# A four-layer stack on one core: stage ends in halves of the tokens, the last FFN in quarters, late gate norms issued before the experts end

## The chip, the cores and the metric

The kernel runs on one core of a Trainium2 chip. The metric is the time of one execution in device microseconds; lower is better. Engines in the profile: PE is TensorE, DVE VectorE, ACT ScalarE, POOL GpSimd, SP SyncE, which here only issues DMAs.

## The reference

x is (4, 512, 128) in float32. Eight blocks follow each other, each on a layernorm of x and added to x:

```python
x = x + _L0_attn_a_ref(_layernorm(x), ...)   # causal softmax attention, 16 heads of 8
x = x + _L0_ffn_ref(_layernorm(x), ...)      # mixture of 8 experts, top 2, and a shared one
x = x + _L0_attn_b_ref(_layernorm(x), ...)   # FAVOR+ linear attention
x = x + _L0_ffn_ref(_layernorm(x), ...)      # the same experts again
x = x + _L1_attn_a_ref(_layernorm(x), ...)   # gated linear attention, 8 heads of 64, own norm inside
x = x + _L1_ffn_ref(_layernorm(x), ...)      # FFN with blockwise FP4 rounding of inputs and weights
x = x + _L1_attn_b_ref(_layernorm(x), ...)   # retention, 16 heads, group norm
x = x + _L1_ffn_ref(_layernorm(x), ...)      # the same FP4 FFN again
```

The FP4 step, on blocks of 16 values of the last dimension, is what the FFN spends its VectorE and GpSimd time on:

```python
scale = jnp.max(jnp.abs(xb), axis=-1, keepdims=True) / 6.0
xn = xb / scale
q = _GRID[searchsorted(_MID, abs(xn))] * sign(xn) * scale   # grid 0, .5, 1, 1.5, 2, 3, 4, 6
```

It is applied to the normed input (512 tokens x 128) and to the product silu(gate) * up (512 x 352) of each batch. Retention's group norm averages over all 512 tokens of a batch, so nothing of a batch's second FFN can start before its retention is complete.

## The kernel before

x stays on the chip as one tile `X`; a batch is 512 tokens, in J = 4 blocks of 128. Softmax attention runs first, in an order written out by hand. Everything after it (about 240 us to the end) is cut into **streams**, one per batch and stage: the experts (`moe`, `shared`, `total`), `inward` and `favor`, `gates`, `keys` and `gated` for the gated attention, then `first` (FFN), `retention`, `leveled` (its group norm and output product) and `second` (FFN with store).

The order in which these are issued comes from a planner, `Clock` (L145). Streams are generators that yield what they wait for and how many PSUM banks they need. Work on ACT, DVE and POOL is registered by `later(engine, us, after, do)`, with a planned duration; whenever an operation's inputs are due it is issued. Among streams that can go on, the planner takes the one that can start first, and then the one with the higher number in the table `FAR` (L39). Engines run their instructions in exactly the planned order, so a waiting instruction holds up all behind it on its engine. The planner's times steer the order; nothing on the chip waits for them.

What the change and the steps of the prediction touch:

- `moments` (L326) computes mean and variance of a batch's four blocks: on DVE two instructions per block (L330, L331). `root_steps` (L305) is three Newton steps for 1/sqrt, on POOL (four instructions a step) or on DVE (three). `centred` (L333) applies scale and offset by four activations on ACT, one per block (L342).
- `add_x` (L402) adds a stage's result from PSUM to the batch's 128x512 of `X` in one DVE instruction (L403).
- `gates(b)` (L970) begins the gated attention: moments, roots on POOL, centring on ACT into `xn`, then transposes on PE (L382). For b = 0 and 1 the stream may start when the FAVOR stage's pools are free; for b = 2 and 3 (`EARLY` = 2) it starts only after the stream `experts`, i.e. when all expert work is issued. That stream runs `rest_pools` (L1115), which sets up the later stages and clears their buffers with five POOL memsets (L1569).
- `project` (L1080) is the gated attention's output product, 16 pairs of block and group into one bank.
- `normed` (L1574) is the norm ahead of `ffn` and `retention`: moments, roots and offset on DVE, centring on ACT.
- `quantized` (L1586) is the FP4 step: block maxima on DVE (L1594 to L1597), division on POOL (L1610), the power of two on DVE (L1600), a step on ACT (L1601), two rounding instructions on DVE (L1605, L1606), and the scale on POOL (L1612).
- `ffn` (L1616) handles a batch: norm, FP4 step on 128x512, transposes, gate and up products per block of 128 tokens, FP4 step on each half (two blocks, 128x704), then per block transposes (L1655), evacuation, down product, one add and, for `second`, one store of 256 KB.
- `leveled` (L1794) ends with four matmuls and one add.
- Retention's scores are masked on POOL, two instructions per head group (L1741).

The kernel also holds a second arm, taken only when decay values leave a range; the measured runs do not take it.

Of the kernel before, what the change touches and what calls it, by code (L numbers as in the profile page):

```python
# [14 lines left out]
ALU = mybir.AluOpType  # L15
# [15 lines left out]
UP = 1.0 + 2.0 ** -22  # L31
EXP, TANH, SILU = ("exp",), ("exp", "silu"), ("silu",)
EARLY = 2

# [4 lines left out]
FAR = {  # L39
    "moe": (34,),  # L40
    "shared": (589, 230, 101, 186, 338, 444, 196, 385),
    "total": (34, 334, 167, 440, 467, 482, 19, 193),
    "in": (0, 0, 100, 527, 450, 482, 45, 323),
    "inward": (364, 104, 384, 461),
    "favor": (378, 171, 133, 588),
    "gates": (135, 468, 451, 231),
    "keys": (237, 481, 541, 82),
    "gated": (377, 269, 540, 166),
    "first": (55, 466, 547, 542),
    "retention": (54, 134, 224, 459),  # L50
    "leveled": (326, 293, 76, 394),
    "second": (75, 76, 343, 438),
}
# [182 lines left out]
class Net:  # L236
    def __init__(self, ctx, tc, d):
# [16 lines left out]
        self.ident = self.k["ident"]  # L254
        self.quantized = None

# [68 lines left out]

    def moments(self, b, mv):  # L326

        for j in range(J):
            st = self.new(self.stat, [P, 6], "bn", bufs=4)
            self.nc.vector.bn_stats(st, self.xi(b * J + j))  # L330
            self.nc.vector.bn_aggr(mv[:, j, :], st)  # L331
# [69 lines left out]

    def add_x(self, b, ps):  # L402
        self.nc.vector.tensor_tensor(self.xb(b), self.xb(b), ps.rearrange("p (j d) -> p j d", d=P), ALU.add)  # L403

# [499 lines left out]
    def front(self, out):  # L904
# [5 lines left out]
        with ExitStack() as ctx, ExitStack() as now, self.tc.tile_pool(name="kept", bufs=1, space=bass.MemoryType.DRAM) as dram:  # L910
# [57 lines left out]
            xs, D, KD = {}, {}, {}  # L968

            def gates(b, clock, gp):  # L970

# [5 lines left out]
                def moments():  # L977
                    self.moments(b, mv[:, b])
                    v = self.new(self.stat, [P, 2, J], "v2")
                    nc.vector.tensor_scalar(v[:, 0], mv[:, b, :, 1], 1e-5, None, ALU.add)  # L980
                    nc.vector.tensor_scalar(v[:, 1], mv[:, b, :, 1], 1.0 + 1e-5, 1e-10, ALU.mult, ALU.add)
                    parts.append(self.root_steps(r12[:, b], v, "r12"))
                    next(parts[0])
# [4 lines left out]

                xn = []
                op = later("pool", 2.8, later("dve", 2.1, clock.since, moments), rest)  # L990
                op = later("act", 2.5, op, lambda: xn.append(self.centred(self.new(gp.mid, [P, J, P], "xn"), b, mv[:, b], r12[:, b, 1], own="g")))
                yield [op], "bank"
                ps = self.turned(xn[0])
# [86 lines left out]
            def project(b, pool, ot):  # L1080
                res = self.centred(self.new(pool, [P, J, P], "res"), b, mv[:, b], r12[:, b, 0], own="p")
                nc.gpsimd.tensor_tensor(self.xb(b), self.xb(b), res, ALU.add)
                ps = self.bank()
                for j in range(J):
                    for p in range(NG):
                        self.mm(ps[:, chunks[j]], ot[:, p, chunks[j]], wo[:, p * P:(p + 1) * P],
                                start=(p == 0), stop=(p == NG - 1))
                return ps

# [3 lines left out]
            with ExitStack() as over, self.banks():  # L1093
# [7 lines left out]
                nc.vector.tensor_scalar(nba, gs[:, :NG], -1.0, None, ALU.mult)  # L1101
                known = {}
                when = lambda *key: lambda: known.get(key)

# [10 lines left out]
                def rest_pools():  # L1115

                    now.close()
                    gp.late = tp(late, "late", 1)
                    gp.rest = self.rest(over, clock, D, KD, out)
                    clock.run("pool", 5.7, clock.since)  # L1120
                    yield 0.0
# [102 lines left out]
                for b in range(B):  # L1224
                    streams[f"inward{b}"] = ([f"favor{b - 2}"] if b >= 2 else [], None, lambda b=b: into(b), 460)
                    streams[f"favor{b}"] = ([f"inward{b}"], "favor", lambda b=b: featured(b), 400)
                    streams[f"gates{b}"] = (["pools" if b < EARLY else "experts"], None, lambda b=b: gates_of(b), 500 - 10 * b)
                    streams[f"keys{b}"] = ([f"gates{b}"] + [f"keys{b - 1}"] * (b > 0), None, lambda b=b: gp.keys(b), 495 - 10 * b)
# [35 lines left out]
    def chunked(self, arm, tp, clock, D, KD, fall, tri, wk, wv, rn, xs, queries, squares, keyed, of_heads, norms, project):  # L1264
# [108 lines left out]
        def steps(b):  # L1373
            yield from before(NG * b)
            done = []
            for u in range(NG * b, NG * (b + 1)):
                yield q[u], "bank", "bank"
                w = scores(u)
                if (u + 1) % NG:
# [3 lines left out]
            yield done, "bank"  # L1383
            ps = project(b, once, D[b])
            yield clock.later("dve", 0.7, [clock.pe(3.7), clock.later("pool", 1.4, clock.later("act", 2.0, clock.since))],
                              lambda: self.add_x(b, ps), "bank")

# [4 lines left out]
    def closed(self, arm, tp, wq, wk, wa, xs, by_token, project):  # L1392
# [87 lines left out]
        for b in range(B):  # L1480
# [3 lines left out]
            for p in range(NG):  # L1484
                attend(b, p, V, ot)
            self.add_x(b, project(b, sm, ot))

# [57 lines left out]
    def rest(self, arm, clock, D, KD, out):  # L1545
# [21 lines left out]
        of_head = va.rearrange("p (j g w) -> p j g w", j=J, w=wide)[:, :, :, :P].rearrange("p j g (i e) -> p j g i e", e=32)[:, :, :, :, :DH]  # L1567
        for t in (va, *ws):
            nc.gpsimd.memset(t, 0.0)  # L1569
        magic = self.new(one, [P, 1], "magic")  # L1570
# [3 lines left out]
        def normed(b, tag):  # L1574

            st, xn = {}, self.new(one, [P, J, P], tag)

            def moments():
                st["mv"] = self.new(self.stat, [P, J, 2], f"mvb{b}")
                self.moments(b, st["mv"])  # L1580
                st["r"] = self.rstd(st["mv"][:, :, 1], f"rstdb{b}", eng=nc.vector)

            op = later("dve", 4.5, clock.since, moments)
            return xn, later("act", 2.0, op, lambda: self.centred(xn, b, st["mv"], st["r"], nc.vector, f"{b}"))

        def quantized(dst, src, n, after, own):  # L1586

            sc, rc = (self.new(one, [P, n // BLK], t + own) for t in ("sc", "rc"))
            tmp = self.new(one, [P, n], "fw" + own)
            blk = lambda t: t.rearrange("p (n k) -> p n k", k=BLK)  # L1590
# [12 lines left out]
            def rounded():  # L1603

                stt(dst, tmp, MAGIC, dst, ALU.add, ALU.add)  # L1605
                stt(dst, tmp, MAGIC, dst, ALU.add, ALU.subtract)  # L1606

            u = n / T
            op = later("dve", 0.8 + 0.7 * u, after, scales)
            op = later("pool", 1.08 * u, op, lambda: nc.gpsimd.tensor_tensor(blk(dst), blk(src), _bc(rc, BLK), ALU.mult))  # L1610
            op = later("act", 0.1 + 0.5 * u, later("dve", 0.42 * u, op, power), number)
            return later("pool", 1.08 * u, later("dve", 1.36 * u, op, rounded), lambda: nc.gpsimd.tensor_tensor(blk(dst), blk(dst), _bc(sc, BLK), ALU.mult))  # L1612

        free = ["a", "b"]

        def ffn(b, store=False):  # L1616
            h, hq = room(KD[b])[:, :J * FF], room(D[b])[:, :J * FF]
            own = free.pop()
            xn, op = normed(b, "xn" + own)
            flat = xn.rearrange("p j d -> p (j d)")  # L1620
            op = quantized(flat, flat, T, op, own)
            yield op, "bank"
            ps = self.turned(xn)
            xT = self.new(one, [P, T], "fw" + own)
            ready = later("act", 0.6, pe(0.5), lambda: nc.scalar.copy(xT, ps), "bank")
            half = J * FF // 2
            halves, ended = [], []

# [15 lines left out]
            for j in range(J):  # L1644
                yield ready, "bank", "bank"
                gates(j)
                if j % 2:
                    c = slice(j // 2 * half, (j // 2 + 1) * half)
                    halves.append(quantized(hq[:, c], h[:, c], half, ended[-2:], f"{own}{j // 2}"))

# [13 lines left out]
            def down(j, hT):  # L1664
# [3 lines left out]
                return pe(0.65)  # L1668

            for i in range(2):  # L1670
                turns = []
                for j in (2 * i, 2 * i + 1):
                    yield halves[i], "bank"
                    turns.append(turn(j))
                for j in (2 * i, 2 * i + 1):
# [6 lines left out]
                    t = down(j, hT)  # L1682

            def add():
                self.add_x(b, po)
                if store:
                    nc.sync.dma_start(out.rearrange("(n p) d -> p n d", p=P)[:, b * J:(b + 1) * J, :], self.xb(b))

            yield later("dve", 0.65, t, add, "bank")
            free.append(own)  # L1690

# [3 lines left out]
        def retention(b):  # L1695
# [22 lines left out]
            for j in range(J):  # L1718
                self.mm(ps1[:, j, :], xs[:, chunks[j]], wv)
            of_v = later("act", 0.65, pe(0.95), lambda: nc.scalar.copy(of_head.rearrange("p j g i d -> p (j g) i d"), ps1.rearrange("p j (g i d) -> p (j g) i d", i=HG, d=DH)), "bank")  # L1720
            yield of_k, "bank"
# [72 lines left out]
        def leveled(b):  # L1794
# [24 lines left out]
            ps2 = self.bank()  # L1819
            for j in range(J):  # L1820
                self.mm(ps2[:, chunks[j]], y[:, chunks[j]], wo)
            yield later("dve", 0.65, pe(0.95), lambda: self.add_x(b, ps2), "bank")

# [29 lines left out]
```

## Time and profile before

| | us |
|---|---|
| median of 3 runs | 1032.96 (1032.49 to 1033.01) |
| the profiled execution | 1032.06 |
| its span, first to last instruction | 1030.3 |
| PE busy | 890.4 |
| DVE busy | 734.2 |
| ACT busy | 560.0 |
| POOL busy | 448.3 |

The costliest groups of the FFN and retention stages, from 640 us to the end, with count, busy time and mean:

| group | count | busy us | mean ns |
|---|---|---|---|
| POOL mask of retention's scores, 128x1024 (L1741) | 32 | 35.4 | 1122 |
| DVE moments per block (L330) | 56 | 14.9 | 267 |
| POOL FP4 division, 128x704 (L1610) | 8 and 8 | 12.1 and 11.8 | 1508 and 1478 |
| POOL FP4 scale, 128x704 (L1612) | 8 and 8 | 11.7 and 11.5 | 1458 and 1443 |
| DVE rounding, 128x704, first (L1605) | 8 and 8 | 7.5 and 7.4 | 944 and 926 |
| DVE rounding, 128x704, second (L1606) | 8 and 8 | 9.1 and 7.1 | 1133 and 893 |
| DVE add to X, 128x512 (L403) | 17 | 11.6 | 684 |

Where two numbers stand, they belong to the two sets of FFN buffers. A row of the timeline reads: start, duration, engine, line, operation, output from inputs, and in brackets how long the engine was idle before it and what released it. PSUM tiles are called `bank` throughout, and a line can be a helper's (L400 is every plain matmul), so groups are told apart by their tiles. Most matmuls stand in the trace as two records, so counts are twice those of the code.

### The profile page before, as it was taken

The page shows a single profiled execution, that of the slowest core. Times are in us where ns is not written, and L with a number is a line of the kernel's source. Part 1 is how long each engine was busy: PE and PEld are TensorE (multiplying, and loading weights), DVE is VectorE, ACT ScalarE, POOL GpSimd, SP SyncE. Part 2 cuts the span into 40 slices and gives each one's busy share as a digit, 9 for nine tenths or more (in the row PEclk, how much of TensorE's full clock was granted, in tenths as well). Part 3 has the DMA queues.
Part 4 walks back from the last instruction along what each step waited for, and adds up shares of the span by engine and source line. Part 5 has one row for each costly group of instructions (what it writes and reads, how often), then busy time and mean ns, then how long its engine had stood idle before and what let it go on. Part 6 is the DMA issues. An engine that isn't in the chain of part 4 may idle for free.

```text
span 1030.3 us, 17949 instructions
## 1 busy us (share of the span) xinstructions
PE 890.4 (86%) x6624; PEld 541.1 (53%) x6624; DVE 734.2 (71%) x1808; ACT 560.0 (54%) x1076; POOL 448.3 (44%) x899
## 2 busy tenths in 40 slices
PE   5999999998999989998988989678798977778734
PEld 3545555554335555444534457446687765566523
DVE  5657777755776898978877755596685864977664
ACT  3556656564774665757476742384345555465422
POOL 2434544341674554555556424463224515343322
PEclk9989999999999999999999999898998997997867
DMA  4000001000000000000000000100000000000000
GB/s 158 2 2 2 2 16 41 2 1 22 0 1 1 1 1 1 2 0 2 11 1 11 1 1 11 32 1 1 1 1 2 1 1 2 1 12 1 12 10 14
DMA packets 8387, 9.82 MB, mean 10 GB/s; under 512 B 1740, under 2 KB 6860, under 8 KB 8036
## 3 DMA queue, kind: packets, MB, share of 16 engines
q1 hardware_dynamic: 8292, 8.60, 2.6%
q8 instruction: 54, 0.88, 0.3%
q14 instruction: 41, 0.34, 0.1%
HBM read 6.50 MB, written 2.10 MB: 8 GB/s over the span
## 4 chain that ended last, share of the span: by engine, by line
PE 53%; DVE 27%; POOL 8%; ACT 7%; issue 4%; DMA 1%; SPq 0%; DVEq 0%; ACTq 0%; POOLq 0%
PE bank L400 48%; DVE D L1015 2%; DVE arg L831 2%; PE bank L382 2%; DVE top L828 1%; DVE h L736 1%; DVE bn L330 1%; DVE D L1606 1%; DVE D L1605 1%; PE bank L1655 1%; DVE top L829 1%; POOL rnt L310 1%; PE bank L492 1%; POOL rstdbe1t L310 1%; DVE den L887 1%
## 5 line engine op out<-in xcount | busy, mean ns | idle before, releaser
L484 DVE TENSOR_REDUCE tops<-bank 128x1 f32<-128x128 f32 (+3 forms) x256 | 110.1, 485 | 55.3 <-PE bank L400 55.2
L400 PE MATMUL bank<-xe,we 128*128 128x512 f32 x256 | 127.6, 620 | 4.5 <-ACT x L737 2.9
L509 ACT ACTIVATE w<-bank 128x512 f32<-128x512 f32 (+1 forms) x192 | 90.5, 526 | 69.5 <-PE bank L400 65.8
L511 POOL TENSOR_SCALAR_AFFINE_SELECT w<-w 128x128 f32<-128x128 f32 x256 | 70.3, 297 | 116.6 <-ACT w L509 116.1
L400 PE MATMUL bank<-qm,kz 32*128 32x384 f32 (+3 forms) x512 | 101.9, 471 | 1.1 <-DVE tops L484 0.6
L400 PE MATMUL bank<-kz,q 32*128 32x512 f32 (+3 forms) x512 | 98.2, 476 | 0.0
L749 POOL TENSOR_TENSOR sum<-sum,y 128x512 f32<-128x512 f32 x56 | 76.7, 1369 | 43.9 <-DVE y L746 41.6
L736 DVE SCALAR_TENSOR_TENSOR h<-h,g 128x512 f32<-128x512 f32 x64 | 60.2, 941 | 21.2 <-ACT g L735 21.1
L400 PEld LDWEIGHTS bank<-xe,we 128*128 128x128 f32 x256 | 43.6, 190 | 49.2 <-issue 29.7
L400 PE MATMUL bank<-h,we 128*128 128x512 f32 x128 | 67.4, 610 | 2.1 <-DVE arg L831 2.1
L735 ACT ACTIVATE h<-bank,half 128x512 f32<-128x512 f32 x64 | 43.8, 684 | 31.6 <-PE bank L400 31.3
L403 DVE TENSOR_TENSOR X<-X,bank 128x512 f32<-128x512 f32 x32 | 21.9, 685 | 50.8 <-PE bank L400 33.0
L400 PE MATMUL bank<-xs,wg 128*128 128x512 f32 x96 | 52.9, 657 | 5.0 <-DVE R L1308 3.3
L400 PEld LDWEIGHTS bank<-kz,q 32*128 32x128 f32 x512 | 38.2, 189 | 32.1 <-issue 11.6
L400 PEld LDWEIGHTS bank<-qm,kz 32*128 32x128 f32 x512 | 47.4, 185 | 13.1 <-DVE tops L484 2.3
L400 PE MATMUL bank<-w,vpad 128*32 128x256 f32 (+3 forms) x512 | 49.0, 449 | 1.8 <-DVE ru L675 1.1
L725 DVE TENSOR_TENSOR xe<-xnT,bank 128x512 f32<-128x512 f32 x64 | 43.2, 678 | 9.9 <-PE bank L400 9.9
L1741 POOL TENSOR_SCALAR_AFFINE_SELECT rw<-rw 128x1024 f32<-128x1024 f32 x32 | 35.4, 1122 | 31.8 <-ACT rw L1740 31.8
L737 ACT ACTIVATE x<-bank,half 128x512 f32<-128x512 f32 x64 | 44.0, 688 | 0.0
L735 ACT ACTIVATE g<-bank,ws 128x512 f32<-128x512 f32 x64 | 43.7, 682 | 0.0
L1740 ACT COPY rw<-bank 128x512 f32<-128x512 f32 x64 | 32.9, 596 | 14.4 <-PE bank L400 14.3
L382 PE MATMUL bank<-ident,xn 128*128 128x128 f32 x80 | 17.5, 314 | 24.9 <-ACT xn L342 19.0
(426 smaller groups left out, 2163.2 us busy)
## 6 DMA issues: line engine op xcount, KB each, us to landing
we<-in_we_dram SPq DMA_DIRECT2D x1, 1536.0 KB, 6.9
wg<-in_wg_dram SPq DMA_DIRECT2D x1, 1280.0 KB, 6.1
X<-in_x_dram SPq DMA_DIRECT2D x4, 256.0 KB, 4.4
kept<-X SPq DMA_DIRECT2D x4, 256.0 KB, 2.5
out_dram<-X SPq DMA_DIRECT2D x4, 256.0 KB, 2.3
wf<-in_wf_dram SPq DMA_DIRECT2D x1, 560.0 KB, 7.5
ws<-in_ws_dram SPq DMA_DIRECT2D x1, 400.0 KB, 4.6
wb<-in_wb_dram SPq DMA_DIRECT2D x1, 320.0 KB, 2.9
```

The lines of the kernel that those rows point to most:

```text
L382: self.nc.tensor.transpose(ps[:, j * P:(j + 1) * P], xn[:, j, :], self.ident)
L400: self.nc.tensor.matmul(out, lhsT=lhsT, rhs=rhs, start=start, stop=stop)
L484: nc.vector.tensor_reduce(top[:, c, 32 * i + r:32 * i + r + 1], ps[i][:, o:o + (c + 1) * P], AX.X, ALU.max)
L509: nc.scalar.activation(w[:, :end], ps[i][:, :end], AF.Exp, scale=scale)
L511: nc.gpsimd.affine_select(out=w[:, o:o + P], in_=w[:, o:o + P], pattern=[[1, P]], compare_op=ALU.is_ge, fill=0.0, base=0, channel_multipli ...
L725: return xe, lambda: tt(xe, xnT[q], ps, ALU.mult)
L735: return (h, x3, lambda: (act(h, ph, AF.Tanh, scale=0.5, bias=half[:, e:e + 1]), act(g, ph, AF.Identity, bias=b1[:, e:e + 1])), lambda: st ...
L736: lambda: stt(h, h, 1.0, g, ALU.add, ALU.mult),
L737: lambda: act(x3, p3, AF.Identity, scale=0.5, bias=half3[:, e:e + 1]))
L749: lambda: nc.gpsimd.tensor_tensor(sums[q], sums[q], y, ALU.add))
L1740: ops = [later("act", 0.6, t, lambda n=n, i=i: nc.scalar.copy(w[n][:, i, :], pp[2 * n + i]), "bank") for i in range(2)]
L1741: ended.append(later("pool", 1.15, ops, lambda flat=flat: nc.gpsimd.affine_select(out=flat, in_=flat, pattern=[[0, 2 * J], [1, P]], compar ...
```

## The change

1. The add at the end of `gated`, `first` and `leveled` is made in two halves of 256 columns (two token blocks each), each followed by the moments of its blocks (`halves`, `add_half`); `known[b]` hands them to the next `normed`, which then only computes roots and offset. `project` and `leveled`'s product are split to match.
2. `normed` centres blocks 0 and 1 on ACT and blocks 2 and 3 on POOL.
3. `gates` for b = 2 and 3 may start when the FAVOR pools are free and its expert total is in; its norm is issued then, with the roots on DVE, and only its transposes wait for `experts`. The five memsets become planned POOL operations.
4. In every FFN but the last one of batch 3, the first half's FP4 step of the product leaves ACT and DVE: after the power of two, three POOL instructions take the place of L1601, L1605 and L1606 (`idle`, `by_pool`).
5. The last FFN of batch 3 (`fine`) does the FP4 step of its input in two halves and that of its product in four pieces of one block. Every `second` adds and stores in two halves.
6. `FAR` has new numbers throughout.

```diff
 FAR = {
-    "gates": (135, 468, 451, 231),
-    "first": (55, 466, 547, 542),
-    "retention": (54, 134, 224, 459),
-    "second": (75, 76, 343, 438),
+    "gates": (326, 327, 150, 502),
+    "first": (139, 90, 381, 419),
+    "retention": (49, 489, 537, 493),
+    "second": (85, 453, 348, 295),
...
+    def add_x(self, b, ps, js=range(4)):
+        x = self.X[:, b * J + js[0]:b * J + js[-1] + 1, :]
+        self.nc.vector.tensor_tensor(x, x, ps[:, js[0] * P:(js[-1] + 1) * P].rearrange("p (j d) -> p j d", d=P), ALU.add)
+
+    def halves(self, clock, b, ps, part, after=0.0):
+        ops = []
+        for i in range(2):
+            if i:
+                yield 0.0
+            ops.append(clock.later("dve", 1.3, [part(i), after], lambda i=i: self.add_half(b, ps, i), "bank" if i else None))
+        yield ops
+
+    def add_half(self, b, ps, i):
+        js = range(2 * i, 2 * i + 2)
+        self.add_x(b, ps, js)
+        if i == 0:
+            self.known[b] = self.new(self.stat, [P, J, 2], f"mvb{b}")
+        self.moments(b, self.known[b], js)
...
-                op = later("pool", 2.8, later("dve", 2.1, clock.since, moments), rest)
-                op = later("act", 2.5, op, lambda: xn.append(self.centred(..., own="g")))
-                yield [op], "bank"
+                xn, eng = [], None if b < EARLY else nc.vector
+                op = later("dve", 2.9, clock.since, moments)
+                op = later("pool" if b < EARLY else "dve", 3.0 if b < EARLY else 1.2, op, rest)
+                op = later("act", 2.0, op, lambda: xn.append(self.centred(..., eng, "g")))
+                yield [op, when("experts") if b >= EARLY else 0.0], "bank"
...
-                    streams[f"gates{b}"] = (["pools" if b < EARLY else "experts"], None, ...)
+                    streams[f"gates{b}"] = (["pools"], None, ...)
...
-        for t in (va, *ws):
-            nc.gpsimd.memset(t, 0.0)
+        zeros = [clock.later("pool", 2.0 if t is va else 1.0, clock.since, lambda t=t: nc.gpsimd.memset(t, 0.0)) for t in (va, *ws)]
...
+            by_act = lambda o, x, r, off: nc.scalar.activation(o, x, AF.Identity, scale=r, bias=off)
+            by_pool = lambda o, x, r, off: nc.gpsimd.tensor_scalar(o, x, r, off, ALU.mult, ALU.add)
+            op = later("dve", 2.4, clock.since, factors)
+            return xn, [later("act", 0.9, op, lambda: centred((0, 1), by_act)), later("pool", 0.7, op, lambda: centred((2, 3), by_pool))]
...
+            def by_pool():
+                nc.gpsimd.tensor_scalar(tmp, tmp, 1.0, MAGIC, ALU.max, ALU.mult)
+                nc.gpsimd.tensor_tensor(dst, tmp, dst, ALU.add)
+                nc.gpsimd.tensor_tensor(dst, tmp, dst, ALU.subtract)
+                scaled(dst, sc)
...
+            if idle:
+                return later("pool", 4.0 * u, op, by_pool)
...
+                i = j if fine else j // 2
+                if fine or j % 2:
+                    c = slice(i * n, i * n + n)
+                    if j % 2 == 0 or not fine:
+                        parts = room_for(2 * FF, f"{own}{j // 2}")
+                    op = quantized(hq[:, c], h[:, c], n, ended[-1] if fine else ended[-2:], parts, i % 2 * FF if fine else 0, not fine and j == 1)
+                    pieces += [op] * (1 if fine else 2)
...
+            def store_half(i):
+                js = slice(2 * i, 2 * i + 2)
+                self.add_x(b, po, range(2 * i, 2 * i + 2))
+                nc.sync.dma_start(to[:, js, :], self.xb(b)[:, js, :])
```

## The prediction

> **What bounds the kernel.** I read the page first, then busy time by stage, then the two stretches of the timeline where TensorE (PE) idles most. The page's engine row, PE's slices and the shares of the chain of waits:
>
> ```profile
> PE 890.4 (86%) x6624; PEld 541.1 (53%) x6624; DVE 734.2 (71%) x1808; ACT 560.0 (54%) x1076; POOL 448.3 (44%) x899
> ...
> PE   5999999998999989998988989678798977778734
> ...
> PE 53%; DVE 27%; POOL 8%; ACT 7%; issue 4%; DMA 1%; SPq 0%; DVEq 0%; ACTq 0%; POOLq 0%
> ```
>
> PE is full for two thirds of the span and half empty at its end; the chain leans on VectorE (DVE) for 27%. By stage (experts, their end, gated attention, FFNs with retention, and from the last retention's output to the end); columns are start:end, length, busy time (count) of each engine, granted clock, DMA:
>
> ```profile
> 240.00:640.00 400.00, 372.67 (x1955) 195.36 (x1956) 305.26 (x614) 239.61 (x421) 202.14 (x351) 0.99 0.01 4
> 640.00:660.00 20.00, 10.48 (x77) 8.64 (x76) 11.25 (x48) 4.67 (x11) 12.84 (x37) 0.83 0.17 48
> 660.00:830.00 170.00, 150.21 (x1230) 117.60 (x1232) 125.50 (x273) 87.75 (x166) 64.67 (x80) 0.92 0.00 1
> 830.00:972.40 142.40, 107.85 (x1174) 83.66 (x1171) 99.44 (x306) 76.53 (x163) 54.70 (x48) 0.84 0.02 5
> 972.40:1030.30 57.90, 25.47 (x115) 19.04 (x113) 33.01 (x85) 14.58 (x35) 14.35 (x10) 0.72 0.04 11
> ```
>
> PE stands still 27.3 us in the experts, 9.5 at their end, 19.8 in the gated stage, 34.5 in the FFN stage, 32.4 in the last 57.9 us. The change adds no matmul, so these are what can be won. Adding up the chain's pieces stage by stage, 63.5 of the 115.5 us it shows from 830 to 972 are DVE: 17.1 of them the rounding (L1605, L1606), 7.4 the moments (L330, L331).
>
> **Part 1, late gates.** The timeline at the experts' end: POOL clears buffers, PE waits for a norm behind them.
>
> ```profile
> 643.32 1.91 POOL L1569 MEMSET rv<- 128x2176 f32 x1 [5.46 <-PE bank L400]
> ...
> 645.17 3.70 POOL L1569 MEMSET rw<- 128x1024 f32 x4
> ...
> 657.77 1.63 PE L382 MATMUL bank<-ident,xn 128*128 128x128 f32 x4 [8.92 <-ACT xn L342]
> ```
>
> Between them stand `offp`, the residual and 12 root steps on POOL. In the built order of the changed kernel the transposes of gates2 follow the last expert total at once; their norm needs only the sixth total and was issued before. Those of gates3 come after five 512-wide matmuls, eight records and three transposes: 5 x 2 records x 0.657 us (row xs,wg) + 1.05 + 0.49 = 8.1 us of PE work. Their norm takes, after its total: add and moments 2.3 us (643.24 to 645.53), four scalar steps 0.8, nine root steps on DVE at 0.2 (the rstd rows: 0.16 and a gap) 1.8, offset 0.2, four centrings 1.65: 6.7 us, covered. So 8.9 us of wait go. The roots put 2 x 2.0 us on DVE, idle 8.7 of these 20 us; without that cover +4. The memsets (5.6 us of POOL) become planned operations ahead of the first mask. SP's order changes little: the third `kept` store still precedes the weight loads, the fourth follows them. Between -9 and -4, I take **-8**.
>
> **Part 2, ends in halves.** One 0.685 us add becomes two of 128x256. The trace has none: by L403 (512: 0.685) and L1637 (352: 0.516) about 0.41, bounds 0.34 and 0.5. DVE pays 0.14 x 14 = 2 us. The norm behind an end waits for add and moments, 989.26 to 991.68 = 2.4 us; with the first half done beside PE's second half, 1.35 stay: -1.07 where PE's second half is long (gated: 3.74 us, the row at 643.04; FFN: its down products), -0.25 after leveled, whose eight records take 1.06 us. Were all twelve on the path: 8 x 1.07 + 4 x 0.25 = -9.6; the chain holds 10.5 us of moments after 640, and a third to a half of that is nearest: **-3** (0 to -9.6).
>
> **Part 3, centring.** ACT's four (1.65 us) become two (0.83) beside two on POOL. No POOL row has that form; nearest is L837 (128x512, 0.65): 0.25 to 0.65 each. Either way POOL ends with ACT or 0.5 later. -0.8 x 12 if always on the path, +0.5 x 12 if POOL's queue is full; the chain holds L342 rarely from 830 on (0.5 us): **-1.5**.
>
> **Part 4, rounding of the first half of seven FFNs on POOL.** DVE loses 7 x (0.93 + 1.0) = 13.5 us, ACT 7 x 0.885. That is 31% of all rounding; of the 27.1 us of it on the chain from 660 to 972, -8.4. POOL gains 7 x (0.65 x 704/512 = 0.89, and twice 1.266 x 704/512 = 1.74, by rows L837 and L1082) = 30.6 us. Each half's own way grows from 0.885 + 1.93 to 4.37, +1.5; all seven on the path: +10.5; PE waits six times for L1612 (19.0 us in all), so I count half: +5. What queues behind the block on POOL are retention's masks, keys' root steps and the other half's scaling.
>
> Here a rule speaks against the change. Row first, POOL and DVE in one stretch, against a normal 0.89 us for L1606:
>
> ```profile
> 979.89 1.99 POOL L1610 TENSOR_TENSOR D<-KD,rcb 128x704 f32<-128x704 f32 x1 [2.70 <-DVE scb L1597]
> ...
> 980.67 1.96 DVE L1606 SCALAR_TENSOR_TENSOR D<-fwb,D 128x704 f32<-128x704 f32 x1
> ```
>
> The Trainium skill ("SBUF — State Buffer", Who interferes with whom) says that a DVE instruction with two SBUF inputs and a GpSimd one that reads SBUF exclude each other for a whole instruction. By the rule, 21 new POOL instructions, each holding up one DVE instruction for half of its 1.46 us at DVE's 70% duty: +10.7 us of DVE, two thirds on the path in a DVE-led stretch, +7. By the row: L1606 averages 1.133 us in the worse group, +0.24 over 0.89; with some 10 such meetings +2.4. Many DVE instructions read PSUM and one SBUF operand, so I take the row. Sum: -8.4 + 5 + 2.4 = **-1** (-8.4 to +17.5).
>
> **Part 5, the last layer.** Before, from the last retention's statistics to the end:
>
> ```profile
> 972.44 0.69 DVE L1786 BATCH_NORM_STATS2 gst<-D 128x6 f32<-128x512 f32 x1 [1.07 <-ACT D L1789]
> ...
> 1002.39 1.12 PE L382 MATMUL bank<-ident,xna 128*128 128x128 f32 x4 [10.09 <-POOL xna L1612]
> ...
> 1004.23 7.01 PE L400 MATMUL bank<-fwT,fwa 128*128 128x352 f32 x16 [0.72 <-ACT fwa L1625]
> ...
> 1025.07 0.69 DVE L403 TENSOR_TENSOR X<-X,bank 128x512 f32<-128x512 f32 x1 [4.73 <-PE bank L400]
> ```
>
> 31.8 us to the gates, of which 4.9 were leveled's root behind second2's rounding. In the new order second0 and nearly all of second2 stand ahead, so the same steps add up to: statistics, means and root 5.7, level 0.85, first half of the matmuls 0.55, adds and moments 2.85, root 2.55, centring 0.9, first half's scales 0.95, POOL 0.54, power, ACT, rounding 1.85, second half's rounding and scaling 1.3, transposes 0.6: 18.7 us. From gates to end, 26.1 before. In quarters DVE does per quarter a product 0.52, reduce 0.51, three small 0.56, power 0.3, rounding 1.0; but the first add of X stands in DVE's order ahead of the third quarter's rounding and waits for two down products (about 13.5 us in). Following the order I get 20.3 us to the last add, then 4.5 as now (store and end): 24.8. Two 128 KB stores in SP's queue replace one, the first hidden. So 57.9 becomes 43.5, -14.4.
>
> The work that made way is not gone: 9.5 us of DVE and 8 of PE move in front. There POOL's order from retention3's first mask to its last holds 31.0 us (eight masks 8.8, two moved roundings 8.7, scalings 13.5), where the masks now run from 948.99 to 968.9, 19.9 us. Fully bound by POOL +11, none if it starts earlier; PE work moved there needs room too: I take +7. **-7.4** (-14.4 to -3).
>
> `FAR` also reorders the expert stage. The counts of expert pieces issued before each stage hardly move (132 to 136 at the gates' pools), so 0, with 5 us either way.
>
> Sum: -8 - 3 - 1.5 - 1 - 7.4 = -20.9 against the profiled execution's 1032.06 us (span 1030.3 and 1.8 around it): 1011.2. The median lies 0.9 higher: **1012 us**.
>
> **Rivals.** (a) DVE was the true bound from 830 on, and POOL, busy 54.7 of 142.4 us, has room: parts 4 and 5 at their good ends, -8 - 3 - 1.5 - 8.4 - 14.4 = -35.3, 998 us. Against it: POOL's 31 us in one stretch. (b) Only part 1 arrives; the tail's saving is spent where its work moved: 1025 us. For it: the same work on engines already 70% busy. (c) POOL becomes the bound of the FFN stage: +10.5 + 7 + 11 = 28.5 us of longer ways, locks and late masks, with parts 2 to 4 winning nothing, against 8 + 14.4 + 1.5: +4.6, 1038 us. It decides once POOL's costs on the path pass 24 us; against it, POOL is under half busy in every stage after 660. (d) The gates' norm is late again behind another wait and all cancels: 1033.
>
> **How the numbers follow.** Forecast 0.45, (a) 0.17, (b) 0.20, (c) 0.13, (d) 0.05. Within 0.2% (2 us) counts as no change, as little as a measurement can tell. Faster: 0.45 + 0.17 + 0.19 = 0.81; same 0.05; slower 0.14. The range reaches just past (a) and to no change: 994 to 1032; the forecast's own is 1003 to 1022.
>
> **What would show it.** Part 1: no PE idle over 3 us before the transposes of `xn`. Part 2: first-half adds before PE's last product. Part 4: the new POOL rows near 0.9 and 1.75 us, DVE under 70% from 660 on, L1606 not above 1.2. Part 5: about 44 us from the last 128x512 statistics to the end. Wrong, if PE waits more for POOL's masks after 900 than 3 us (the waits now name them for 0.4), or the expert stage alone moves by over 5 us.

## The result and the profile after

| | before | after |
|---|---|---|
| median of 20 runs each, us | 1032.7 (1030.2 to 1033.6) | 1034.4 (1032.4 to 1038.5) |
| ratio after / before | | 1.002, 95% 1.0012 to 1.0027 |
| profiled execution, us (span) | 1032.06 (1030.3) | 1036.2 (1033.7) |

The change made the kernel 0.2% slower; the prediction was 1012 us, and its range ended at 1032. The page of the changed kernel, in the lines shown of before:

```profile
PE 896.5 (87%) x6624; PEld 542.8 (53%) x6624; DVE 739.8 (72%) x1851; ACT 544.0 (53%) x1049; POOL 492.8 (48%) x922
...
PE   5999999999999987899889999779997994857745
...
PE 55%; DVE 25%; POOL 9%; ACT 6%; issue 4%; DMA 0%; SPq 0%; DVEq 0%; POOLq 0%; ACTq 0%
```

The same matmuls take PE 6 us more, DVE has not fallen although 13.5 us of rounding left it, and POOL has gained 44.5 us. The chain is as before: PE, then DVE. By the same stages (start:end, length, busy time and count of PE, weight loads, DVE, ACT, POOL; granted clock, DMA share, GB/s), the last two cut at this kernel's own last group statistics, 984.6 us:

```profile
240.00:640.00 400.00, 370.58 (x1876) 192.73 (x1876) 301.58 (x622) 235.75 (x417) 192.84 (x335) 0.96 0.01 4
640.00:660.00 20.00, 19.25 (x122) 14.98 (x120) 9.07 (x23) 5.76 (x11) 9.83 (x17) 0.91 0.00 0
660.00:830.00 170.00, 150.75 (x1370) 116.81 (x1371) 132.15 (x318) 90.30 (x166) 86.09 (x106) 0.96 0.02 6
830.00:984.60 154.60, 110.52 (x1084) 84.69 (x1082) 111.31 (x313) 64.23 (x143) 94.17 (x77) 0.82 0.02 6
984.60:1033.70 49.10, 22.83 (x86) 17.02 (x86) 25.39 (x91) 10.64 (x27) 11.09 (x15) 0.63 0.04 10
```

Two things go the predicted way. Of the two late norms, the one whose transposes of `xn` PE waited 8.9 us for is now ready when the last expert total ends. The transposes of the other, at 671.75 us, wait 3.6 us: DVE works through the norm of an FFN (661.70 to 666.87) before it begins the moments of the late one. And the tail after the last statistics is 49.1 us instead of 57.9; 43.5 was predicted.

But the last expert total now ends at 661.1 us, before it ended at 643.2; and the last statistics come at 984.6, before at 972.4. So 17.9 us are lost before the gain of part 1 begins, and 12.2 before that of part 5. One more mark proved useful, the gated attention's output product of the last batch (`wg,D`), since batch 3 is the last through every later stage. It starts at 837.1 before and 847.2 after. The timeline of PE in the kernel before shows the last expert total and this product (start, duration, engine, line, operation; a wait would stand in brackets):

```profile
642.04 1.16 PE L400 MATMUL bank<-ident,sum 128*128 128x128 f32 x8
...
837.07 2.23 PE L400 MATMUL bank<-wg,D 128*128 128x128 f32 x12
```

In the changed kernel, with the transposes of the two late norms between them:

```profile
659.90 1.16 PE L401 MATMUL bank<-ident,sum 128*128 128x128 f32 x8
...
660.90 0.60 PE L383 MATMUL bank<-ident,xn 128*128 128x128 f32 x4
...
671.75 1.48 PE L383 MATMUL bank<-ident,xn 128*128 128x128 f32 x4 [3.56 <-ACT xn L343]
...
847.16 2.06 PE L401 MATMUL bank<-wg,D 128*128 128x128 f32 x17
```

Below, "last gated product" is its start, and the time from there to the span's end is the last batch's own way. The other suspect is POOL. Its timeline in the changed kernel before the last statistics, start, duration, engine, line, in brackets the idle time before it:

```profile
968.58 1.09 POOL L1815 TENSOR_SCALAR_AFFINE_SELECT rw<-rw 128x1024 f32<-128x1024 f32 x1
970.23 2.56 POOL L1648 TENSOR_SCALAR fwa<-fwa 128x704 f32<-128x704 f32 x1 [0.56 <-DVE fwa L1638]
972.87 1.66 POOL L1649 TENSOR_TENSOR D<-fwa,D 128x704 f32<-128x704 f32 x1
974.62 1.66 POOL L1650 TENSOR_TENSOR D<-fwa,D 128x704 f32<-128x704 f32 x1
976.36 1.38 POOL L1645 TENSOR_TENSOR D<-D,sca 128x704 f32<-128x704 f32 x1
977.70 1.39 POOL L1645 TENSOR_TENSOR D<-KD,rca 128x704 f32<-128x704 f32 x1
979.04 1.10 POOL L1815 TENSOR_SCALAR_AFFINE_SELECT rw<-rw 128x1024 f32<-128x1024 f32 x1
```

Almost no brackets: POOL does not pause from 951 to 980 but for 0.6 us. The new instruction L1648 takes 2.6 us where I had 0.89, and the last mask (979.04) stands behind two whole blocks of rounding, begun at 951.1 and 970.2.

### The profile page after: what moved, and what is told of

Same layout as the page of the kernel before. It is cut to its first block, busy times and chain, and to the rows that moved or that the text cites. A ratio compares the mean times of both kernels' runs of the same rounds, so it can differ in the third digit from the quotient of the medians.

```text
span 1033.7 us, 18017 instructions
## 1 busy us (share of the span) xinstructions
PE 896.5 (87%) x6624; PEld 542.8 (53%) x6624; DVE 739.8 (72%) x1851; ACT 544.0 (53%) x1049; POOL 492.8 (48%) x922
## 4 chain that ended last, share of the span: by engine, by line
PE 55%; DVE 25%; POOL 9%; ACT 6%; issue 4%; DMA 0%; SPq 0%; DVEq 0%; POOLq 0%; ACTq 0%
PE bank L401 50%; DVE bn L331 2%; DVE D L1038 1%; DVE den L906 1%; POOL D L1645 1%; DVE X L405 1%; PE bank L383 1%; DVE h L755 1%; DVE arg L850 1%; DVE fwa L1638 1%; PE bank L511 1%; POOL D L1649 1%; POOL D L1650 1%; POOL rw L1815 1%; POOL w L530 1%
## 5 line engine op out<-in xcount | busy, mean ns | idle before, releaser
L401 PE MATMUL bank<-xe,we 128*128 128x512 f32 x256 | 129.8, 630 | 0.0
L768 POOL TENSOR_TENSOR sum<-sum,y 128x512 f32<-128x512 f32 x56 | 79.3, 1416 | 60.8 <-DVE y L765 58.7
L401 PE MATMUL bank<-h,we 128*128 128x512 f32 x128 | 69.5, 627 | 1.1 <-DVE arg L850 1.0
L744 DVE TENSOR_TENSOR xe<-xnT,bank 128x512 f32<-128x512 f32 x64 | 43.3, 678 | 20.7 <-PE bank L401 20.7
L405 DVE TENSOR_TENSOR X<-X,bank 128x256 f32<-128x256 f32 (+1 forms) x48 | 24.0, 503 | 37.6 <-PE bank L401 35.2
L1815 POOL TENSOR_SCALAR_AFFINE_SELECT rw<-rw 128x1024 f32<-128x1024 f32 x32 | 36.5, 1162 | 15.6 <-ACT rw L1814 15.6
L767 POOL TENSOR_TENSOR y<-y,x 128x512 f32<-128x512 f32 x20 | 25.4, 1268 | 27.5 <-ACT y L766 27.2
```

What stands on the lines that cost most here:

```text
L401: self.nc.tensor.matmul(out, lhsT=lhsT, rhs=rhs, start=start, stop=stop)
L405: self.nc.vector.tensor_tensor(x, x, ps[:, js[0] * P:(js[-1] + 1) * P].rearrange("p (j d) -> p j d", d=P), ALU.add)
L744: return xe, lambda: tt(xe, xnT[q], ps, ALU.mult)
L768: lambda: nc.gpsimd.tensor_tensor(sums[q], sums[q], y, ALU.add))
L1815: ended.append(later("pool", 1.15, ops, lambda flat=flat: nc.gpsimd.affine_select(out=flat, in_=flat, pattern=[[0, 2 * J], [1, P]], compar ...
```

## The experiments

Theory POOL: the 21 rounding instructions on POOL hold up masks and scalings and eat the gains. Rival, theory expert stage: the new order up to 661 us loses, and POOL matters little. Ratios are to the kernel before, run beside each on the same chip.

**The rounding back, order kept.**

```diff
             def by_pool():
-                nc.gpsimd.tensor_scalar(tmp, tmp, 1.0, MAGIC, ALU.max, ALU.mult)
-                nc.gpsimd.tensor_tensor(dst, tmp, dst, ALU.add)
-                nc.gpsimd.tensor_tensor(dst, tmp, dst, ALU.subtract)
+                number()
+                rounded()
                 scaled(dst, sc)
```

> The changed kernel in its own planned order, but with the rounding of the first halves back on ACT and DVE (three instructions at the place of the three POOL ones). Theory POOL: the 41.7 us that these 21 instructions take on POOL (2.6 + 1.7 + 1.7 per block) stand in front of retention's masks and the scalings between 889 and 920 and between 957 and 980; without them PE's half-empty slices there fill, the last statistics of a retention (984.6 us in the changed kernel) come 8 to 15 us earlier, DVE's power-of-two rows fall from 1.0 back to about 0.6 us, and the time is 1018 to 1026 us. Theory expert stage: the loss lies before 661 us, where the experts end 18 us later than before; then nothing changes, 1032 to 1036 us.

Measured 1027.7 us, ratio 0.9953 (0.993 to 0.9976), 6.9 us under the changed kernel (1.002 - 0.9953 = 0.0067 of 1032). The last statistics came at 977.7, 6.9 us earlier. PE's wait for POOL's scaling between 900 us and the last statistics, in the changed kernel and then in this one:

```profile
PE bank L1722 <- POOL D L1645: 12.3, 4, 5.6
```

```profile
PE bank L1721 <- POOL D L1645: 3.8, 1, 3.8
```

Columns: total, times, longest. So POOL's part is real, but it is a third of the 22 us between forecast and result, and the experts end at 662.3 here too.

**The centring back as well, order kept.** The two `by_pool` centrings become `by_act`.

> As the run before, and also blocks 2 and 3 of each norm are centred on ACT again, in the same order. If the centring on POOL was worth its 1.5 us, this is 1 to 2 us slower than the run before; if POOL's queue was the limit and 11.3 us of centring stood in it, 1 to 4 us faster.

Measured 1031.9 us, 0.9992 (0.998 to 1.0004): 4.0 us slower than the run above. Centring on POOL is worth more than I gave it; its rows last 0.45 to 0.55 us.

**The rounding back, planned anew.** The `idle` argument is left out.

> Rounding of the first halves on ACT and DVE, and the planner told so: the order after the first FFN is planned anew. Theory POOL: as the first run or up to 5 us better, 1013 to 1026 us. Theory expert stage: 1032 to 1036 us, since the order up to 661 us is the changed kernel's.

Measured 1040.0 us, 1.0072 (1.0049 to 1.0096): beyond both expectations, 12 us slower than the same work in the kept order. The experts' end is the same (663.0), the tail is 57.9 us again. An order planned anew moves the time as much as any part of this change does.

**Part 1 alone**, on the kernel before with its old table.

> The kernel before with nothing but the late gates' norm ahead of the experts' end and the planned memsets, the old table. My step: 8 us less, 1025 us, no PE idle over 3 us ahead of the transposes of xn. Rival: the norm's instructions among the experts and a changed order cost there what the hole gave, 1031 to 1036 us.

Measured 1038.7 us, 1.0064 (1.0039 to 1.0088), 6 us slower. The norms were early, with no wait before their transposes, yet the planner put the last of these at 691 us (before: 669.5), and the last gated product started at 841.3. In another order, planned anew too, the part comes out 9 us to the good (e11), so neither run alone sizes it.

**The first rounding step on ACT**, the two sums on POOL. In this kernel `number()` stands in place of L1648 without adding its constant back, so the rounding leaves out that addition; the count and size of instructions are what is measured.

> The changed kernel in its own order, with only the first of the three POOL instructions of each block (the maximum and product, 2.6 us each on POOL) made by ACT as before; the two sums stay on POOL. Theory POOL: 7 x 2.6 = 18 us less on POOL, of a total of 41.7; the run with all three back gained about 7 us on the changed kernel, so this one gains 3 to 5: 1029 to 1031 us. Rival, the lock between POOL's two-input instructions and DVE is what costs: the sums stay, so no gain, 1033 to 1036 us.

Measured 1029.4 us, 0.9971 (0.996 to 0.9982): 5.1 us of the 6.9, for 18.3 of the 41.8 us on POOL. This points to the long instruction more than to the two sums; the intervals of this run and of e1 overlap, so the share of the sums is not sized.

**The new table alone, and the old table with all the rest.**

```diff
 FAR = {
-    "moe": (34,),
-    "shared": (589, 230, 101, 186, 338, 444, 196, 385),
...
+    "moe": (105,),
+    "shared": (104, 152, 283, 484, 275, 86, 77, 326),
...
```

> The kernel before with nothing but the changed kernel's table FAR. I predicted 0 with 5 us either way. If the expert stage's new order is what loses, its end comes 15 us or more later than in the kernel before (643 us) and the time is 1036 us or more; if the order only trades, 1028 to 1038 us.

Measured 1053.1 us, 1.0201 (1.0184 to 1.0218): the table alone costs 20.7 us. The experts end at 659.9.

> The changed kernel with the old table FAR. If the new table's order of the expert stage loses 5 us or more, this is 1025 to 1030 us; if the order is as good as another, or suits the new parts better, 1033 to 1042 us.

Measured 1006.5 us, 0.9781 (0.9729 to 0.9834), four runs of which one took 1016.6; repeated below. This is the decisive pair: the table costs 21 us on the old kernel and 25 on the new one, and everything else that the change does is a gain of some 2%. The windows of this kernel, its last two cut at its own last statistics, 947.0:

```profile
240.00:640.00 400.00, 375.18 (x1978) 198.70 (x1978) 303.07 (x622) 240.78 (x424) 201.20 (x352) 0.99 0.01 4
...
830.00:947.00 117.00, 86.64 (x1050) 66.59 (x1048) 95.11 (x248) 60.13 (x129) 75.41 (x63) 0.91 0.02 5
947.00:1004.50 57.50, 29.80 (x126) 22.04 (x124) 41.87 (x116) 16.24 (x40) 24.20 (x23) 0.78 0.05 14
```

In the first row PE is busy 4.6 us longer than in the changed kernel, at a granted clock of 0.99 for 0.96. Busy time by clock gives 371.4 us of full-speed work by 640 us against 355.8: 15.6 us, give or take 4, since the clock is printed to two places. The experts end 14.9 us earlier (646.2 for 661.1). The last statistics come at 947.0 for 984.6, and the last gated product here:

```profile
822.64 1.95 PE L401 MATMUL bank<-wg,D 128*128 128x128 f32 x16
```

**The last FFN whole**, `FINE = 0`, new table.

> The changed kernel without the finer last FFN (that one too takes its first half's rounding on POOL then). From the last 128x512 statistics to the end the changed kernel takes 49 us, the kernel before 58; if the quarters make half of that, it is 53 to 55 us here and the time 1038 us or more; if the quarters' work in front costs what they save, 1032 to 1036 us.

Measured 1039.9 us, 1.0077 (1.006 to 1.0094), 5.9 us slower than the changed kernel; the tail is 53.6 us. Half of the shorter tail is lost again, and the last statistics come at 983.5, no earlier to speak of than 984.6, so the work moved in front costs little. This is not the last FFN of the kernel before, though: left whole, it too takes its first half's rounding on POOL (see part 5 below).

**Which entries of the table.** e9 keeps the old entries from `moe` to `gated` and takes the new ones of the last four stages; e13 takes old entries for `moe`, `shared`, `total` and `in` alone; e14 for `inward`, `favor`, `gates`, `keys` and `gated` alone.

> The changed kernel with the old numbers of FAR for the experts, FAVOR and the gated attention, and the new ones for first, retention, leveled and second. With the whole old table the time was 1006 us, with the whole new one 1034 us. If the order of the experts and the gated attention is what loses, 1003 to 1011 us; if that of the last four stages, 1025 to 1036 us.

Measured 1010.6 us, 0.9792 (0.9776 to 0.9809). The late entries are harmless.

> The changed kernel with the old numbers of FAR for moe, shared, total and in only. The last batch's gated output product stays late in PE's order (row 2737 of the build; 2742 with the new table, 2644 with the old). Theory last gated product: it starts after 838 us and the time is 1024 to 1040 us. Rival, the order of the experts' own pieces loses: 1004 to 1014 us.

> The changed kernel with the old numbers of FAR for inward, favor, gates, keys and gated only; the experts' entries stay new. The last batch's gated output product stands early in PE's order (row 2648). Theory last gated product: it starts at 820 to 830 us and the time is 1002 to 1014 us. Rival, the experts' own order: 1024 to 1036 us.

Measured 1050.0 us, 1.0161 (1.0123 to 1.02), for e13, slower than the upper end expected: experts' end 668.4, last gated product 859.7. And 1036.2 us, 1.0037 (1.0019 to 1.0054), for e14. That is the time of its rival (the experts' own order), but e13 speaks against that rival, since it has the old expert entries and is slower still. In e14 the last gated product stands early in PE's order, yet starts late:

```profile
846.68 2.03 PE L401 MATMUL bank<-wg,D 128*128 128x128 f32 x16
```

Its experts end at 656.8, and the transposes of the late gates run at 676.1 and 686.8 us, where the old table has 649.5 and 670.9. From the experts' end to the product PE has the same 1304 matmul records as in e17 and needs 189.9 us for 176.5. Its largest wait there, total, times, longest (7.4, 2, 4.4 in e17):

```profile
PE bank L1683 <- POOL xnb L1645: 14.7, 2, 11.7
```

These are an FFN's transposes waiting for POOL's scaling. So the place in the order alone does not decide, and neither half of the early entries heals the loss: they work only together.

**The parts in the old table's order.** e11 is without part 1, e12 without the finer last FFN (both planned anew, so they differ from e17 in more than the part); e15 makes each add and its moments whole after the second half, e16 centres on ACT, e10 and e18 round on ACT and DVE (all in the order kept). e17 is e7 again, on one chip with e18.

> The changed kernel with the old table, in its own order, with the rounding of the first halves back on ACT and DVE at the same place. If part 4 costs as in the new order (about 7 us), 997 to 1002 us; if POOL has room for it in this order, or DVE (75% busy here) needs the relief, 1005 to 1013 us.

> The changed kernel with the old table and without part 1: the late gates wait for the experts, their roots on POOL, the memsets at once, planned anew. My step was 8 us: 1012 to 1016 us. The run of part 1 alone was 6 us slower than the kernel before: if the part itself loses, 998 to 1003 us.

> The changed kernel with the old table and without the finer last FFN. My step was 7.4 us: 1012 to 1016 us. Rival: from the last 128x512 statistics to the end this order takes 57.5 us with the quarters, as long as the kernel before (57.9), so they bring nothing here and the gain lies ahead of them: 1004 to 1009 us.

> The changed kernel with the old table, in its own order, but the add of X and all four blocks' moments in one go after the second half. My part 2 was 3 us (0 to 9.6): 1009.5 us (1006 to 1016). Rival, nothing on the path: 1004 to 1008 us.

> The changed kernel with the old table, in its own order, all four blocks of a norm centred by ACT. My part 3 was 1.5 us: 1008 us. In the new order the same step was worth 4 us: 1010.5 us. If POOL's queue is the limit, faster, 1002 to 1005 us.

> The changed kernel with the old table once more: 1006 to 1012 us, 2 to 2.6% under the kernel before.

> The same with the rounding of the first halves back on ACT and DVE, on the same chip. If part 4 costs in this order what it costs in the new one, 4 to 8 us under the run before; if DVE needed the relief there, equal or slower.

| run | us | ratio (95%) | experts' end | last gated product | from there to the end |
|---|---|---|---|---|---|
| before | 1032.7 | 1 | 643.2 | 837.1 | 193.2 |
| after | 1034.4 | 1.002 (1.0012 to 1.0027) | 661.1 | 847.2 | 186.5 |
| e17, old table | 1008.3 | 0.9783 (0.9751 to 0.9815) | 646.2 | 822.7 | 181.6 |
| e11, without part 1 | 1018.7 | 0.9873 (0.9852 to 0.9893) | 644.8 | 836.3 | 181.5 |
| e12, last FFN whole | 1018.2 | 0.9852 (0.9825 to 0.9879) | 645.3 | 823.9 | 192.6 |
| e15, ends whole | 1017.7 | 0.9865 (0.9828 to 0.9902) | 645.2 | 823.1 | 185.3 |
| e16, centring on ACT | 1018.1 | 0.9843 (0.9799 to 0.9887) | 650.5 | 833.3 | 185.9 |
| e10, rounding on ACT and DVE | 1006.8 | 0.9749 (0.9718 to 0.978) | 650.4 | 826.5 | 177.7 |
| e18, the same again | 1006.3 | 0.9745 (0.9726 to 0.9764) | 647.5 | 823.8 | 180.8 |

The last three columns are of the profiled execution (spans). e11 loses 13.6 us up to the start of the last gated product and nothing behind it; e12 loses 11.0 us behind it and next to nothing before. Single runs of these kernels spread over 3 to 11 us, so e15 and e16 hold their signs but hardly their sizes; e15's profiled span is only 4 us above e17's, and in e16 4.3 us of the difference lie before the experts' end, where nothing but spread is expected. Part 4 is at best even: e18 and e17 overlap, e10 agrees with e18. **Both e17 and e18 beat both kernels**, by 2.2 and 2.5% of the kernel before; e18 is the version to take, if only by its smaller spread.

## Why the prediction was wrong

**The step that failed is the last term of the sum**: "`FAR` also reorders the expert stage. The counts of expert pieces issued before each stage hardly move (132 to 136 at the gates' pools), so 0, with 5 us either way." The runs show +20.7 us (e6) and +24.5 (after against e17: 1.002 - 0.9783). Without it my terms add to -20.9, and the runs with the old table give -22.4. That these agree is partly luck: the sizes found below for parts 1 to 5 add to -27.2, with two parts much larger than forecast and one of the other sign. I counted how much expert work was issued and not which batch's: the new order brings the first two group statistics forward (804.6 and 843.7 us, in e7 821.0 and 861.8) and the last back (984.6 for 947.0). The last gated product stood 98 rows later in PE's built order (2742 for 2644), which was to be seen before any run, though e14 shows that this row alone would not have been enough.

How the table's 24.6 us at the last gated product arise is shown in part: 14.9 are there at the experts' end, with less PE work done at a lower clock; the other 10 come between that end and the product, where PE does 1587 matmul records in the changed kernel for 1304 in e17, other work first. Which single entries do it stays open; neither the experts' nor the attention's entries do it alone. On the kernel before, the same table loses elsewhere: in e6 the last gated product starts only 9.0 us later (846.1), and the way behind it is 11.7 us longer (204.9). That part of the loss was not traced.

Point by point, sizes from the old table's order as differences of ratios times 1032:

**Part 1**, predicted -8: -9.3 (e11 against e17), but +6 alone (e4), and all these orders were planned anew. What is shown is the wait. The first late transposes, in e11 and then in e17:

```profile
661.10 1.63 PE L383 MATMUL bank<-ident,xn 128*128 128x128 f32 x4 [10.63 <-ACT xn L343]
```

```profile
649.49 0.66 PE L383 MATMUL bank<-ident,xn 128*128 128x128 f32 x4
```

Its sign (no PE idle over 3 us there) came true in e17 but not in the changed kernel. The other late norm, which I had as 6.7 us and covered by 8.1 us of PE work, gave its first block only some 10 us after the last total, behind another norm on DVE, and PE waited 3.56 us. Why the part alone cost 6 us was not separated.

**Part 2**, predicted -3 (0 to -9.6): -8.5 by the ratios, -4 by the profiled spans. Inside its bounds.

**Part 3**, predicted -1.5 (-9.6 to +6): -6.2 here with the uncertainty named above, -4.0 in the new order. Too small, and the prediction misread its own chain. It gave L342 0.5 us from 830 us on; the chain of before holds 4.6 (start, duration):

```profile
889.74 1.66 ACT rn L342 x4
957.89 1.25 ACT xnb L342 x3
994.29 1.66 ACT xna L342 x4
```

Half of that is already 2.3 us. The total of 115.5 us from 830 to 972 also leaves out ACT and POOL; with them the chain's pieces come to some 135, and DVE's 63.5 are under half of them.

**Part 4**, predicted -1: +6.9 in the new order (e1), +3.9 in the old (e18 against e17, overlapping). Two terms were mis-sized. POOL's three instructions take 5.97 us a block, not 4.37: the row chosen for L1648 (L837, 0.65 us for 512 columns) doesn't carry over to a maximum with a product. And the lock: I weighed a rule of the Trainium skill ("SBUF — State Buffer", Who interferes with whom) at +10.7 us of DVE against a row's +2.4 and took the row. With the order kept, taking 13.9 us of rounding off DVE lowered its busy time by only 3.9 us (743.7 in e1, 739.8 after), so 10 us came back as longer instructions; in the old order 12.0 us went off and busy time rose from 745.0 to 752.1, so 19 came back. The rule was the nearer one. Two signs said so as well: the second rounding (L1643 now) took 1.35 us on average in the worse group, over the 1.2 named, and DVE was 72% busy from 660 us on, over 70%.

**Part 5**, predicted -7.4 (-14.4 for the tail, +7 for the work in front): -7.1 (e12 against e17), -5.9 in the new order (e8). Near in sum, but these runs do not size the quarters. Left whole, the last FFN of e8 and e12 rounds its first half on POOL, and PE waits longer for it than in the kernel before. Its transposes of the product, in e8 and then before:

```profile
1024.72 1.54 PE L1722 MATMUL bank<-ident,D 128*128 128x128 f32 x6 [12.34 <-POOL D L1645]
```

```profile
1018.72 1.54 PE L1655 MATMUL bank<-ident,D 128*128 128x128 f32 x6 [7.48 <-POOL D L1612]
```

The difference, 4.9 us, may be most of the 5.9. From the first gate product to the end the changed kernel takes 27.4 us (from 1006.27), before 26.1; 24.8 was forecast. The 8.8 us by which the tail shrank lie ahead of that product: 21.7 us for 31.8 before (18.7 forecast), and e8 has the same 21.7 without quarters. So in this order the quarters show no gain over the last FFN of the kernel before. A whole last FFN with its rounding on ACT and DVE was not run, so what they are worth stays open. In the old table's order the tail is 57.5 us with quarters, with other work beside it, and 65.1 without.

Rival (d), 1033 us, came nearest the time, but by luck: the gates' norm was late by 3.6 us, not by enough to cancel everything. Nor does (c), POOL as the bound (1038 us), hold: POOL's rounding costs 7 us, far from the 24 at which it was to decide. Of the signs that I named, the expert stage moved by 18 us, over the 5 that would mean "wrong", and PE's wait for masks after 900 us was 1.4 us, under the 3 named: the first pointed to the table, the second away from the masks. (The 0.4 us named for before is another tile, `w` at L1325, at 833 us; after 900 us no wait of before names the masks.)

## What to carry to other kernels

A table that steers an order is a change like any other: take it back alone before explaining what the rest does, and judge a part only inside one kept order, since planning anew moved this kernel by 12 us. When batches pass through the same stages, follow the last batch's entry into the last long chain (here its gated product): it and the length behind it showed where each run lost, while busy totals did not. And check what a part's absence brings back: e8 and e12 took the quarters out and put a POOL block in. Of the work moved from DVE to POOL here, 10 us of 13.9 came back to DVE in one order and 19 us for 12.0 in the other, as longer instructions.

## What was not expected of the hardware

**DVE instructions with one input got longer too.** I had counted only two-input ones. Rows of e17, with the rounding on POOL, then of e18, the same order without it (count | busy us, mean ns | idle before):

```profile
L1638 DVE TENSOR_SCALAR fwa<-D 128x704 uint32<-128x704 uint32 x6 | 4.3, 711 | 1.3 <-POOL D L1645 1.3
L1635 DVE TENSOR_SCALAR sca<-sca 128x44 f32<-128x44 f32 x6 | 3.5, 580 | 0.0
```

```profile
L1638 DVE TENSOR_SCALAR fwa<-D 128x704 uint32<-128x704 uint32 x6 | 3.1, 517 | 0.0
L1635 DVE TENSOR_SCALAR sca<-sca 128x44 f32<-128x44 f32 x6 | 0.7, 122 | 0.0
```

The same instruction takes 1.4 and 4.8 times as long. In the new table's order the means are 1148 and 615 ns in the changed kernel, 663 and 213 in e1; but L1638 on the other buffer, `fwb`, has 946 and 956, so not every row moves. The same section of the Trainium skill says that `tensor_scalar` can run in a mode that takes the shared port pair and then excludes GpSimd; these rows agree, though no run here shows which mode was taken.

**A maximum with a product on POOL** over 128x704 took 2.6 us, 3.7 ns a column; a product with a sum (L837, 128x512) 0.65, 1.3 ns a column. Starts of neighbours bear it out: 970.23 to 972.87.

**The granted clock was lower with the new expert entries.** From 240 to 640 us it was 0.94 to 0.97 in the eight profiled kernels that have them, and 0.97 to 1.00 in the other twelve. At 0.96 for 0.99, 3% of 375 us of matmuls are 11 of the 15 us that the experts end later, an estimate with the same error of about 4 us. In the changed kernel PE was busy 5.85 us from 490 to 500 us and was granted 0.66, with no pause over 3.2 us; in e17 it was busy throughout there, at 1.00. Two things limit the reading. From 240 to 250 us the changed kernel was granted 0.51 with PE always busy, but e7 and e17, one and the same kernel, were granted 1.00 and 0.83 there, so part of it changes from one execution to the next. And e13 was granted 0.98 up to 640 us and its experts ended last of all, at 668.4. Why the new order is granted less wasn't tried.
